# Two adapter layers on one core: outer Strassen-Winograd sums with one operand in PSUM, fixed PSUM banks, and another order of transposes

## The chip, the cores and the metric

The kernel runs on one core of a Trainium2 chip. The metric is the device time of one execution in microseconds; the figure for a kernel is the median of several executions. A separate profiled execution gives the trace, with its own time.

## The reference

128 samples `x[b]` of 128 rows by 1024 columns pass through two layers. In each layer every sample has one of three roles (`itok_B_1_2`, clipped to 0..2), and the role chooses the weights:

```python
h = jnp.einsum('bsh,bhk->bsk', hidden_states, W_down[role]) + b_down[role][:, None, :]
h = jax.nn.gelu(h, approximate=False)
u = jnp.einsum('bsk,bkh->bsh', h, W_up[role]) + b_up[role][:, None, :]
y = hidden_states + u
mean = jnp.mean(y, axis=-1, keepdims=True)
var = jnp.mean(jnp.square(y - mean), axis=-1, keepdims=True)
yn = (y - mean) * jax.lax.rsqrt(var + LN_EPS)
return yn * gamma[role][:, None, :] + beta[role][:, None, :]
```

The second layer is the same with its own weights and reads the first layer's result. Everything is fp32; the inner width is 512.

## The kernel before, in words

The samples are sorted by role on the chip. `perm` holds the order, and 14 groups of eight samples with one role (the octets) are taken together; the few left over go in pairs and singles. A layer has three stages: the left-over items (`PlainItem`), the 14 octets (`Octet`), which make `gelu(x W_down)` transposed and store it to DRAM, and the up stage (`Up`), 65 items that make the second product, the residual sum and the normalization.

**An octet** multiplies the 1024-wide transposed input of eight samples by `W_down`. It does so with two levels of the Winograd form of Strassen's product. The outer level cuts the input into four blocks: A11 and A12 are the first and second half of the 1024 features for samples 0 to 3, A21 and A22 the same for samples 4 to 7. A block is 128 partitions by 2048 numbers (four feature tiles of 512 columns). The input arrives by DMA in a ring of five `staged` buffers (`Turns.load`), and VectorE transposes it in 32x32 squares into the blocks (`Turns.turn`, L557): two instructions of 128x512 for each sample, `k=0` for the first half of the features and `k=1` for the second. Seven blocks exist (`take_block`, `give_block`).

From the four blocks, `Octet.outer` (L651 to L662) makes four outer sums: s3 = A11 - A21, A21 = A21 + A22 in place, s2 = A22 - s3 and s4 = A12 - s2. Each is two instructions of 128x1024; the last half of s4 is GpSimd's, the other seven are VectorE's. Seven outer products B11, B21, T2, T1, T3, B22, T4 (the list `ORDER`) follow, with A11, A12, s2, A21, s3, s4, A22 as left operands (`LEFT`). All but T3 are cut again: GpSimd makes four inner sums d0 to d3 of 128x512 for each (`inner`, L674 to L683), TensorE multiplies seven inner products p1 to p7 (`product`, order `PS`), each two matmuls of 256 columns. T3 is multiplied plainly in eight steps of 512 columns.

**The inner products meet in PSUM.** p1, p3, p5 and p7 add into a "b" bank, p4 and p6 into an "e" bank, and p2 into an "x" bank, into which ScalarE first copies what p1 left (`carry`, L716). `flow` (L734 to L744) takes each finished result out of PSUM, mostly by VectorE, which adds it to `results`, and for B11 by ScalarE copies (L732). As p7 adds to the same bank as p5, it may only start when the flow between them has read the bank. `after` applies the gelu on ScalarE (L722).

**The order of all work is written by hand.** `at(time, step)` puts a step into one list by a nominal time, and the list is run through in order of time, which fixes the order of instructions on each engine; every engine then works in that order and waits only for data. In `Octet.steps`, `put(t, f)` counts in slots of one inner product. An octet is 50 slots: product q begins at slot 0, 7, 14, 21, 28, 36, 43, and its p1 to p7 are two slots apart, so that two outer products are always interleaved. The transposes of the eight samples stand at slots -28 to -4, the outer sums at -1.4 (s3), 3 (s2), 9 (A21) and 15 (s4), the inner sums from 5.6 slots ahead of each product.

**PSUM** has eight banks: a pool gives the tags "b", "e" and "a" three, three and two of them in rotation (`bank`, L143 to L146). The plain items take four banks at a time, the up stage also runs on b, e and a.

**Jobs beside the octets.** The weights of the other two roles are prepared while octets 0 to 11 run: `DownJob` (four sums of 128x1024 at L398, then 24 of 128x256 at L363 to L366) in octets 0 to 3, and three `UpJob` (four sums each at L398) in octets 4 to 11.

Of the kernel before, what the change touches and what calls it, by code (L numbers as in the profile page):

```python
# [10 lines left out]
F32 = mybir.dt.float32  # L11
# [16 lines left out]
def kernel(  # L28
# [113 lines left out]
    nc.gpsimd.memset(zero, 0.0)  # L142
    BANKS = {"b": 3, "a": 2, "e": 3}  # L143

    def bank(t, tag):
        return psum.tile([P, 512], F32, tag=t, name=f"{t}{tag}", bufs=BANKS[t])  # L146

# [3 lines left out]
    def zeros(tags):  # L151
        for t in tags:
            cleared(bank(t, "_zero"))

# [22 lines left out]

    ps = bank("a", "row_ps")
    nc.tensor.matmul(ps[:, 0 : B + 2 * R], ones[0:1, 0:P], row[0:1], start=True, stop=True)
# [66 lines left out]
    def gathered(name, values):  # L246
        ps = bank("a", name + "_ps")
        nc.tensor.matmul(ps[0:SQ, 0:B], values, onehot, start=True, stop=True)
        t = const.tile([1, B], I32, name=name)
        nc.vector.tensor_copy(t, ps[0:1, 0:B])  # L250
        return t, ps
# [122 lines left out]
    class DownJob:  # L374
# [20 lines left out]

        def sum(self, name):
            a, b = {"T1": ("B12", "B11"), "T2": ("B22", "T1"), "T3": ("B22", "B12"), "T4": ("B21", "T2")}[name]
            tt(self.at[name], self.at[a], self.at[b], sub)  # L398

# [3 lines left out]
        def steps(self, start, end):  # L403

            s = [(start - 0.1, self.begin)] + [(start + 0.8 * q, lambda q=q: self.load(q)) for q in range(NQ)]
            work = [(1.0, lambda name=name: self.sum(name)) for name in ("T1", "T2", "T3", "T4")]
            for k, q in enumerate(INNER):
                for op in range(4):
                    work.append((0.35, lambda q=q, k=k, op=op: inner_sums(self.at[q], self.extra[k % 3])[op]()))
                work.append((0, lambda q=q, k=k: self.store(q, k % 3)))  # L410
            work += [(0, lambda q=q: self.store(q, None)) for q in PLAIN]
            t, pace = start + 6, (end - start - 6) / sum(w for w, _ in work)
            for w, step in work:
                s.append((t, step))
                t += w * pace
            return s
# [7 lines left out]
    class UpJob:  # L424
# [18 lines left out]
        def steps(self, start, end):  # L443
            s = [(start - 0.1, self.begin)] + [(start + q, lambda q=q: self.load(q)) for q in range(2)]
            t, pace = start + 6, (end - start - 6) / 4
            for name in ("T1", "T2", "T3", "T4"):
                s.append((t, lambda name=name: DownJob.sum(self, name)))
                t += pace
            for k, name in enumerate(ORDER):
                s.append((end + 0.6 * k, lambda name=name: self.store(name)))  # L450
            return s
# [120 lines left out]
    class PlainItem:  # L572


        def __init__(self, layer, slots, nth, early=False):
            self.layer, self.slots, self.nth, self.early = layer, slots, nth, early
            self.parity = parity = nth % 2
            self.tag = f"p{layer}_{slots[0]}"
            self.turns = Turns(layer, slots)
            self.n = len(slots) * P  # L580
            self.tags = ["e", "b", "a", "e"] if parity else ["b", "e", "a", "b"]

# [9 lines left out]
        def prepare(self):  # L592
            self.bias = new_bias(self.layer, None if self.slots[0] < 2 else self.slots[0], self.tag)
            first = turn_of["results"] % 2
            k = (first, 1 - first, 2)[self.nth % 3]
            self.h = results[:, ts(k, 2048)][:, 0 : 4 * self.n].rearrange("p (f c) -> p f c", f=4)
            self.ps = [bank(t, self.tag + str(f)) for f, t in enumerate(self.tags)]

# [31 lines left out]
    class Octet:  # L630
        def __init__(self, layer, g):
            self.layer, self.g = layer, g
            self.slots = [2 + 8 * g + s for s in range(8)]
            self.tag = f"o{layer}_{g}"
            self.turns = Turns(layer, self.slots)
            self.b = {}
            self.flows = {}

# [6 lines left out]
        def turn(self, s, k):  # L645
            i, c = divmod(s, 4)
            if c == 0:
                self.take(f"A{i + 1}{k + 1}")
            self.turns.turn(s, k, self.b[f"A{i + 1}{k + 1}"][1], c * P)

        def outer(self, name, half, engine):  # L651

            o, a, b, op = {
                "s3": ("s3", "A11", "A21", sub),
                "A21": ("A21", "A21", "A22", add),
                "s2": ("s2", "A22", "s3", sub),
                "s4": ("s4", "A12", "s2", sub),
            }[name]
            if o not in self.b:
                self.take(o)  # L660
            o, a, b = (self.b[n][1][:, ts(half, 2)] for n in (o, a, b))
            engine.tensor_tensor(o, a, b, op)  # L662

        LEFT = {"B11": "A11", "B21": "A12", "T2": "s2", "T1": "A21", "T3": "s3", "B22": "s4", "T4": "A22"}

# [27 lines left out]
        def product(self, q, p):  # L693
            ps, d = self.ps.setdefault(q, {}), self.d[q]
            m = lambda ii, kk: self.m(q, ii, kk)
            if p == "p1":
                ps["b"] = bank("b", self.tag + q)
            elif p == "p4":
                ps["e"] = bank("e", self.tag + q)
            t, w, v = {  # L700
# [10 lines left out]
        def carry(self, q):  # L711
            ps = self.ps[q]
            ps["x"] = bank("a", self.tag + q)
            if self.g == 0 and q in ("B11", "B21"):
                cleared(ps["x"])
# [43 lines left out]
        def plain_step(self, q, k):  # L759
            ps = self.ps.setdefault(q, {})  # L760
            f, j = divmod(k, 4)
            if j == 0:
                ps[f] = bank("e", f"{self.tag}{q}{f}")
            nc.tensor.matmul(
# [34 lines left out]
        def steps(self, base, turns=True):  # L799
# [3 lines left out]
            self.d = {}  # L803
            if turns:
                for s in range(8):
                    t = -28 + 3.3 * s
                    turning.append((base + 0.5 * t, lambda s=s: self.turns.load(s)))
                    for k in range(2):
                        put(t + 0.8 * k, lambda s=s, k=k: self.turn(s, k))
            put(-0.6, self.begin)  # L810
            starts, _ = self.starts()
            put(starts["B21"] - 1, self.begin_0)
            for t, name in ((-1.4, "s3"), (3, "s2"), (9, "A21"), (15, "s4")):
                for half in range(2):
                    engine = nc.gpsimd if name == "s4" and half else nc.vector
                    put(t + 2.2 * half, lambda n=name, h=half, g=engine: self.outer(n, h, g))
            gone = {"A11": ("B11",), "A12": ("B21",), "s2": ("T2",), "A21": ("T1",), "s3": ("T3",), "s4": ("B22",), "A22": ("T4",)}
            for q in ORDER:
                b = starts[q]
                put(b + 13.6, lambda q=q: self.give(self.LEFT[q]))  # L820
                if q in PLAIN:
# [48 lines left out]
    class Up:  # L870
# [40 lines left out]
        def seeded(self, t):  # L911
            ps = bank(t, self.tag)
            if self.m < 3:
                cleared(ps)
# [3 lines left out]
        def products(self):  # L918
# [7 lines left out]
            def s2():  # L926
                ps["a"] = bank("a", self.tag)
                product(ps["a"], A(0, 1), "B21", self.place, True)
                self.end(0, 0, ps["a"])
# [31 lines left out]

            seeds = [(-4, lambda: self.seeded("b")), (1.5 if self.ns == 2 else -0.5, lambda: self.seeded("e"))]
            if self.ns == 2:
# [18 lines left out]
        def finish_last(self):  # L982
# [29 lines left out]
            def begin_bank(item, s, cols, t):  # L1012
                begun[item.m, cols.start] = ps = bank(t, f"{item.tag}_end{cols.start}")
                nc.scalar.copy(ps, item.t["beta"][:, cols])
# [114 lines left out]
    for layer in range(2):  # L1129
# [6 lines left out]
        for kind, n in items:  # L1136
# [6 lines left out]
            else:  # L1143
# [12 lines left out]
                for s in range(len(slots)):  # L1156
                    turning.append((base - lead + 1.7 * s, lambda item=item, s=s: item.turns.load(s)))
                    for k in range(2):
                        at(base - lead + 1.7 * s + 0.4 * k, lambda item=item, s=s, k=k: item.turn(s, k))
                if not first:  # L1160
                    idx = LEFT.index(slots[0])

                    def load(item=item, idx=idx, layer=layer, slot=slots[0], only=None):
                        if not only:
                            item.r = reg(role_at, slot, [ENG.SP], R - 1)
                        c = reg(left_changed, idx, [ENG.SP], 1) if idx >= 2 else None
                        parts = 1 if only is None else 4
                        load_raw(layer, item.parity, item.r, [nc.sync], parts=parts, cond=c, only=only)

# [7 lines left out]
        turning.sort(key=lambda v: v[0])  # L1177
        for k, (time, step) in enumerate(turning):
            when = max(time - 9, turning[k - NSTAGED][0] + 0.45) if k >= NSTAGED else time - 5
            loaded = max(when, loaded)  # L1180
# [30 lines left out]

        o_at = oct_base[0][1]
        job_1 = DownJob(layer, 1, five_blocks, nc.scalar)
        for time, step in job_1.steps(begun_at + 15, o_at - 26):
# [35 lines left out]


        up_base = []
        for m in range(NSEQ):
# [107 lines left out]
```

## Time and profile before

| | us |
|---|---|
| median of three runs (3126.56 to 3132.67) | 3126.98 |
| the profiled execution | 3125.19 |
| its span on the core | 3123.1 |
| layer 0: up to the first product of octet 0 | 155.0 |
| layer 0: the 14 octets | 641.8 |
| layer 0: up stage | 773.2 |
| layer 1: up to the first product of octet 0 | 131.8 |
| layer 1: the 14 octets | 636.4 |
| layer 1: up stage and end | 784.8 |

The time is that of the whole execution, the span what the core's records cover; 2.1 us lie around it. The stage borders were read from the first matmul of the tiles of each octet (for octet g they are named bo_gB, eo_gB, ao_gB and bo_gT, eo_gT, ao_gT in the trace). Engines are PE (TensorE), PEld (its weight loads), DVE (VectorE), ACT (ScalarE), POOL (GpSimd) and SP (which issues the DMAs). A row of a group gives count, busy time and the mean duration of one instruction; an entry in square brackets in a timeline is the idle time ahead of an instruction and what ended it.

| octet, from p1 to the next octet's p1 | layer 0, us | layer 1, us |
|---|---|---|
| 0 | 50.46 | 47.55 |
| 1 | 48.59 | 46.54 |
| 2 | 48.31 | 47.67 |
| 3 | 46.69 | 46.69 |
| 4 to 12, mean | 44.87 | 44.89 |
| shortest of these | 43.88 | 43.88 |

### The profile page before, as it was taken

Reading aid. Unit: us, or ns where it says so; the run is one execution under the profiler, and the core shown is the slowest. Engines: PE = TensorE matmul, PEld = TensorE weight load, DVE = VectorE, ACT = ScalarE, POOL = GpSimd, SP = SyncE. Lnnn points to the kernel's source line nnn. Section 1 sums busy time; section 2 is a strip of 40 time slices with the busy share of each in tenths; the row PEclk is TensorE's granted clock in tenths of the full one; section 3 lists DMA queues with packets and bytes.
Section 4 is the critical chain, followed back from the end, with each engine's and each line's share of the span. In section 5 each row is a group of like instructions: output and inputs, shape, how many; then the busy total and the mean of one; then the engine's idle time right before and its main releaser. Section 6 shows DMA issues by size and latency. Waiting matters only on the chain. (4 is left out here: it accounts for less than half of the span.)

```text
span 3123.1 us, 40323 instructions
## 1 busy us (share of the span) xinstructions
PE 3027.9 (97%) x9953; PEld 1872.6 (60%) x9953; DVE 2434.8 (78%) x3802; ACT 1160.2 (37%) x2576; POOL 2195.6 (70%) x1593
## 2 busy tenths in 40 slices
PE   7889999999999999999998999999999999999999
PEld 6776777778544444444477777778774444444443
DVE  4489989888677777777764899898966777777777
ACT  1122222222445455545421222222224545454544
POOL 0087888898577776777601988888886777767775
PEclk8999999999999999999999999999999999999999
DMA  8765658766667676866688566677658666777665
GB/s 190 219 169 165 195 184 251 210 189 206 246 219 219 221 257 236 281 217 221 220 223 251 140 200 187 198 227 224 186 178 282 216 223 215 269 251 256 216 222 176
DMA packets 350014, 675.42 MB, mean 216 GB/s; under 512 B 35661, under 2 KB 232526, under 8 KB 342618
## 3 DMA queue, kind: packets, MB, share of 16 engines
q1 hardware_dynamic: 338914, 658.63, 68.0%
q10 hardware_dynamic: 10872, 14.22, 1.3%
q8 instruction: 85, 1.39, 0.2%
q14 instruction: 143, 1.17, 0.1%
HBM read 669.55 MB, written 247.49 MB: 294 GB/s over the span
## 5 line engine op out<-in xcount | busy, mean ns | idle before, releaser
L864 PE MATMUL bu<-wall,blocks 128*128 (+1 forms) x2016 | 907.6, 592 | 0.0
L864 PEld LDWEIGHTS bu<-wall,blocks 128*128 128x128 f32 x2016 | 383.0, 190 | 479.6 <-issue 478.2
L1077 POOL TENSOR_TENSOR varu<-varu,mhalf 128x1 f32<-128x1 f32 x254 | 329.9, 1299 | 421.4 <-ACT varu L1076 416.4
L864 PE MATMUL eu<-wall,blocks 128*128 (+1 forms) x1008 | 473.7, 592 | 0.0
L557 DVE STREAM_TRANSPOSE blocks<-staged 128x512 f32<-128x512 f32 x512 | 341.4, 690 | 132.8 <-DMA staged<-in_x_dram 66.5
L1084 DVE SCALAR_TENSOR_TENSOR units<-blocks,meanu,results 128x1024 f32<-128x1024 f32 x249 | 319.8, 1284 | 79.7 <-ACT units L1075 79.5
L662 DVE TENSOR_TENSOR blocks<-blocks 128x1024 f32<-128x1024 f32 x196 | 339.5, 1735 | 0.0
L864 PEld LDWEIGHTS eu<-wall,blocks 128*128 128x128 f32 x1008 | 191.5, 190 | 240.7 <-issue 211.2
L677 POOL TENSOR_TENSOR units<-blocks 128x512 f32<-128x512 f32 x84 | 123.3, 1468 | 291.7 <-DVE blocks L557 257.1
L722 ACT ACTIVATE results<-results,bcolo 128x256 f32<-128x256 f32 x392 | 207.2, 538 | 317.0 <-DVE results L744 286.9
L1071 ACT ACTIVATE partu<-statu 128x2 f32<-128x2 f32 x254 | 51.6, 203 | 716.2 <-DVE blocks L980 711.4
L674 POOL TENSOR_TENSOR units<-blocks 128x512 f32<-128x512 f32 x168 | 265.2, 1578 | 66.0 <-PE bo_3B L689 6.0
L1092 POOL TENSOR_TENSOR units<-units,results 128x1024 f32<-128x1024 f32 x125 | 295.4, 2364 | 2.5 <-ACT units L1091 2.5
L1075 ACT ACTIVATE units<-blocks,meanu 128x1024 f32<-128x1024 f32 x250 | 287.1, 1148 | 8.5
L683 POOL TENSOR_TENSOR units<-blocks,units 128x512 f32<-128x512 f32 x168 | 276.7, 1647 | 6.6
L1094 DVE SCALAR_TENSOR_TENSOR units<-units,varu,results 128x1024 f32<-128x1024 f32 x128 | 279.3, 2182 | 0.0
L972 DVE TENSOR_TENSOR blocks<-bu,blocks 128x512 f32<-128x512 f32 x252 | 173.3, 688 | 133.4 <-PE bu L864 133.4
L864 PE MATMUL au<-wall,blocks 128*128 (+1 forms) x504 | 236.8, 592 | 0.0
L857 POOL TENSOR_TENSOR blocks<-blocks 128x256 f32<-128x256 f32 x126 | 207.5, 1647 | 26.7 <-PE eu L864 26.7
L980 DVE SCALAR_TENSOR_TENSOR blocks<-bu,blocks 128x512 f32<-128x512 f32 x250 | 171.9, 688 | 49.9 <-PE bu L864 49.9
L680 POOL TENSOR_TENSOR units<-units,blocks 128x512 f32<-128x512 f32 x84 | 140.8, 1677 | 62.8 <-PE bo_1T L689 5.0
L864 PEld LDWEIGHTS au<-wall,blocks 128*128 128x128 f32 x504 | 95.8, 190 | 119.4 <-issue 119.0
(779 smaller groups left out, 5274.3 us busy)
## 6 DMA issues: line engine op xcount, KB each, us to landing
staged<-in_x_dram SPq DMA_DIRECT2D x512, 128.0 KB
mid<-units SPq DMA_DIRECT2D x128, 512.0 KB
staged<-mid SPq DMA_DIRECT2D x512, 128.0 KB
blocks<-in_x_dram SPq DMA_DIRECT2D x126, 512.0 KB
blocks<-mid SPq DMA_DIRECT2D x126, 512.0 KB
out_dram<-units SPq DMA_DIRECT2D x125, 512.0 KB
hq<-results SPq DMA_DIRECT2D x56, 1024.0 KB
blocks<-hq SPq DMA_DIRECT2D x112, 512.0 KB
```

What stands on the lines that cost most here:

```text
L557: nc.vector.transpose(to[:, :, at_col : at_col + P].rearrange("p j (a t) -> p j a t", t=SQ), v[:, ts(k, 4)])
L662: engine.tensor_tensor(o, a, b, op)
L674: engine.tensor_tensor(d["d1"], m(0, 0), m(1, 0), sub)
L683: engine.tensor_tensor(d["d2"], m(0, 1), d["d0"], sub)
L722: nc.scalar.activation(y, y, AF.Gelu, bias=self.bias[:, f : f + 1])
L857: engine.tensor_tensor(dst[:, 1], a11, a21, sub)
L864: nc.tensor.matmul(ps, a[:, j], wu(w, place, j), start=start and j == 0, stop=j == 1, skip_group_check=True)
L1075: nc.scalar.activation(box["o"], self.x[:, s], AF.Square, bias=m, accum_out=v)
L1077: nc.gpsimd.tensor_tensor(v, v, mhalf[:, 0:1], ALU.pow)
L1084: nc.vector.scalar_tensor_tensor(box["o"], self.x[:, s], box["m"][:, 0:1], self.t["gamma"], add, mul)
L1092: nc.gpsimd.tensor_tensor(o, o, self.t["beta"], add)
L1094: nc.vector.scalar_tensor_tensor(o, o, v, self.t["beta"], mul, add)
```

## The change

Outer sums. They go sample by sample (128 partitions by four runs of 128 columns), 16 instructions of 512 elements in place of eight of 1024. For samples 4 to 7 the transpose of the first half (A21 as it comes) is written to a PSUM bank instead of a block, and s3 and A21 read it there. For s2, ScalarE copies the sample's piece of A22 into a PSUM bank, and for s4 (made in place in A12) it copies s2 of samples 4 and 5; the last two pieces of s4 are GpSimd's with all operands in SBUF.

Order. From octet 1 on, samples 0 to 3 are transposed at slots -42.5 to -30 and samples 4 to 7 at -22 to -5; s3 stands at slots -15 to -4, A21 at -8.2 to -1.2, s2 at 0 to 5.1, s4 at 22 to 27. Octet 0 has slots of its own. The jobs' sums are cut in halves of 512.

Banks. Eight tiles are held for good, and each role has a fixed set: in the octets b has three, e two (was three), x one (was two), and two are for the raw transposes and ScalarE's copies.

```diff
-    BANKS = {"b": 3, "a": 2, "e": 3}
...
+    all_banks = [psum.tile([P, 512], F32, tag=f"bank{k}", name=f"bank{k}", bufs=1) for k in range(8)]
+    BANKS = {"b": (0, 1, 2), "e": (3, 4, 5), "a": (6, 7), "de": (3, 4), "dt": (5, 7)}
+    bank_turn = dict.fromkeys(BANKS, 0)
+
+    def bank(t):
+        k = BANKS[t][bank_turn[t] % len(BANKS[t])]
+        bank_turn[t] += 1
+        return all_banks[k]
...
-        def sum(self, name):
+        def sum(self, name, half):
             a, b = {"T1": ("B12", "B11"), "T2": ("B22", "T1"), "T3": ("B22", "B12"), "T4": ("B21", "T2")}[name]
-            tt(self.at[name], self.at[a], self.at[b], sub)
+            n = self.at[name].shape[1] // 2
+            o, a, b = (self.at[k][:, ts(half, n)] for k in (name, a, b))
+            tt(o, a, b, sub)
...
-            self.ps = [bank(t, self.tag + str(f)) for f, t in enumerate(self.tags)]
+            self.ps = [all_banks[k] for k in ((2, 3, 4, 6), (5, 7, 0, 1))[self.parity]]
...
         def turn(self, s, k):
             i, c = divmod(s, 4)
+            if i and k == 0:
+                self.raw21[s] = v = bank("dt").rearrange("p (j c) -> p j c", c=P)
+                self.turns.turn(s, k, v, 0)
+                return
...
+        def copied(self, name, s):
+
+            self.copy[s] = v = bank("dt").rearrange("p (j c) -> p j c", c=P)
+            nc.scalar.copy(v, self.at_sample(name, s))
+
+        def outer(self, name, s, apart=True):
+
+            v = lambda n: self.at_sample(n, s)
+            if name == "s3":
+                tt(v("s3"), v("A11"), self.raw21[s], sub)
+            elif name == "A21":
+                tt(v("A21"), self.raw21[s], v("A22"), add)
+            elif name == "s2":
+                tt(v("s2"), self.copy[s], v("s3"), sub)
+            elif apart:
+                tt(v("A12"), v("A12"), self.copy[s], sub)
+            else:
+                nc.gpsimd.tensor_tensor(v("A12"), v("A12"), v("s2"), sub)
+
+        LEFT = {"B11": "A11", "B21": "A12", "T2": "s2", "T1": "A21", "T3": "s3", "B22": "A12", "T4": "A22"}
...
-                ps["e"] = bank("e", self.tag + q)
+                ps["e"] = bank("de")
...
-            ps["x"] = bank("a", self.tag + q)
-            if self.g == 0 and q in ("B11", "B21"):
+            ps["x"] = all_banks[6]
+            if self.g == 0 and q == "B11":
                 cleared(ps["x"])
...
-                    t = -28 + 3.3 * s
-                    turning.append((base + 0.5 * t, lambda s=s: self.turns.load(s)))
-                    for k in range(2):
-                        put(t + 0.8 * k, lambda s=s, k=k: self.turn(s, k))
+                    if early:
+                        first, second, s3, a21 = (
+                            (-42.5 + 1.8 * s, -36 + 2 * s, None, None)
+                            if s < 4
+                            else (
+                                (-22, -21, -15, -8.2), (-19.5, -18.5, -13.5, -7.4), (-11, -7, -6, -2.5), (-9.5, -5, -4, -1.2)
+                            )[s - 4]
+                        )
+                    else:
+                        t = -29 + 3.3 * s if s < 4 else -13.2 + 2.6 * (s - 4)
+                        first, second, s3, a21 = t, t + 0.8, t + 1.7, max(t + 2.4, -8.2 + 0.8 * (s - 4))
+                    turning.append((base + 0.5 * first, base + 0.5 * second, lambda s=s: self.turns.load(s)))
+                    for t, k in zip((first, second), (0, 1) if s < 4 else (1, 0)):
+                        put(t, lambda s=s, k=k: self.turn(s, k))
+                    if s >= 4:
+                        put(s3, lambda s=s: self.outer("s3", s))
+                        put(a21, lambda s=s: self.outer("A21", s))
...
-            for t, name in ((-1.4, "s3"), (3, "s2"), (9, "A21"), (15, "s4")):
-                for half in range(2):
-                    engine = nc.gpsimd if name == "s4" and half else nc.vector
-                    put(t + 2.2 * half, lambda n=name, h=half, g=engine: self.outer(n, h, g))
...
+            for s in range(4, 8):
+                t = ((-1.4, 0, 2, 3.7) if self.g else (1.2, 2.4, 3.6, 4.8))[s - 4]
+                put(t, lambda s=s: self.copied("A22", s))
+                put(t + 1.4, lambda s=s: self.outer("s2", s))
+                t = 21 + 1.6 * (s - 4)
+                if s < 6:
+                    put(t, lambda s=s: self.copied("s2", s))
+                put(t + 1.3, lambda s=s: self.outer("A12", s, s < 6))
             for q in ORDER:
                 b = starts[q]
-                put(b + 13.6, lambda q=q: self.give(self.LEFT[q]))
+                if q != "B21":
+                    put(b + 13.6, lambda q=q: self.give(self.LEFT[q]))
...
-            if self.m < 3:
+            if self.m < 4:
                 cleared(ps)
...
-            seeds = [(-4, lambda: self.seeded("b")), (1.5 if self.ns == 2 else -0.5, lambda: self.seeded("e"))]
+            seeds = [({0: -3.4, 37: -2.9}.get(self.m, -4), lambda: self.seeded("b")), (1.5 if self.ns == 2 else -0.5, lambda: self.seeded("e"))]
...
-        for k, (time, step) in enumerate(turning):
-            when = max(time - 9, turning[k - NSTAGED][0] + 0.45) if k >= NSTAGED else time - 5
+        for k, (time, _, step) in enumerate(turning):
+            when = max(time - 9, turning[k - NSTAGED][1] + 0.05) if k >= NSTAGED else time - 5
...
+        at(o_at - 0.1, lambda: bank_turn.update(b=0, de=1))
```

## The prediction

> **What bounds the kernel now.** I read the busy shares first, then the stages, the octets one by one, TensorE's waits inside an octet, and last what VectorE and GpSimd do at those moments. The page's first row, and busy time by stage (columns: length of the stretch; then busy us and instructions of each engine; the TensorE clock; DMA):
>
> ```profile
> PE 3027.9 (97%) x9953; PEld 1872.6 (60%) x9953; DVE 2434.8 (78%) x3802; ACT 1160.2 (37%) x2576; POOL 2195.6 (70%) x1593
> 155.00:796.80 641.80, 615.25 (x2569) 486.69 (x2568) 562.40 (x852) 168.36 (x405) 544.76 (x354) 0.99 0.64 193
> 796.80:1570.00 773.20, 773.20 (x1820) 345.11 (x1819) 588.84 (x894) 387.95 (x827) 541.82 (x432) 1.00 0.72 237
> 1701.80:2338.20 636.40, 613.86 (x2569) 486.48 (x2568) 561.15 (x852) 168.80 (x405) 545.78 (x354) 0.99 0.68 193
> ```
>
> TensorE is the bound. In the up stage (second row) it never pauses, so no VectorE work saved can show there. In the two octet stages it is idle for 26.6 and 22.5 us by the records, while VectorE is 88% and GpSimd 85% busy. The change is in these stages. Single octets:
>
> ```profile
> 254.05:302.36 48.31, 44.33 (x185) 34.46 (x184) 47.67 (x72) 12.01 (x29) 37.96 (x25) 1.00 0.59 188
> 529.55:575.14 45.59, 44.20 (x186) 34.55 (x184) 42.00 (x62) 12.00 (x29) 38.76 (x25) 1.00 0.73 226
> 708.99:752.88 43.89, 43.39 (x185) 34.88 (x184) 37.90 (x60) 12.09 (x29) 38.24 (x25) 1.00 0.50 145
> ```
>
> Octet 2, with the DownJob's sums, is VectorE's: 47.67 of 48.31 us. Octets 8 and 12 are not, but still lose something to waits. TensorE's timeline shows the floor and the losses:
>
> ```profile
> 575.14 1.03 PE L689 MATMUL bo_9B<-blocks,wall 128*128 128x256 f32 x4
> 594.13 1.03 PE L689 MATMUL bo_9T<-units,wall 128*128 128x256 f32 x4
> 541.18 1.13 PE L689 MATMUL bo_8B<-blocks,wall 128*128 128x256 f32 x4 [0.42 <-DVE results L734]
> 544.70 1.10 PE L689 MATMUL bo_8B<-units,wall 128*128 128x256 f32 x4 [0.67 <-DVE results L744]
> 597.37 1.13 PE L689 MATMUL bo_9T<-units,wall 128*128 128x256 f32 x4 [0.49 <-POOL units L680]
> ```
>
> The first two rows are 22 slots apart without a wait between: 18.99 / 22 = 0.863 us a slot, so 50 slots are 43.2 us. 28 octets would take 1209; they take 641.8 + 636.4 = 1278.2. All that this change can win is about 69 us. The other rows name the two culprits: a flow of VectorE that came late, near an octet's start, and GpSimd's d0 for T1 at slot 25. What the two engines do then:
>
> ```profile
> 538.62 2.17 DVE L662 TENSOR_TENSOR blocks<-blocks 128x1024 f32<-128x1024 f32 x1
> 540.72 0.41 DVE L734 TENSOR_TENSOR results<-bo_8B,results 128x256 f32<-128x256 f32 x1
> 541.89 2.33 DVE L662 TENSOR_TENSOR blocks<-blocks 128x1024 f32<-128x1024 f32 x1
> 544.15 0.41 DVE L744 TENSOR_TENSOR results<-bo_8B,results 128x256 f32<-128x256 f32 x1
> 543.10 2.25 POOL L683 TENSOR_TENSOR units<-blocks,units 128x512 f32<-128x512 f32 x1
> 548.87 2.35 POOL L662 TENSOR_TENSOR blocks<-blocks 128x1024 f32<-128x1024 f32 x1
> ```
>
> Each late flow sits right behind an outer sum of more than 2 us; TensorE's two waits end when it is read. And the sums are this long only in company:
>
> ```profile
> L662 DVE TENSOR_TENSOR blocks<-blocks x196: 1182/1948/2343, 163.1 to 2306.9; 128x1024 f32<-128x1024 f32 x196
> L683 POOL TENSOR_TENSOR units<-blocks,units x168: 1262/1526/2312, 152.8 to 2330.4; 128x512 f32<-128x512 f32 x168
> L557 DVE STREAM_TRANSPOSE blocks<-staged x512: 661/698/714, 18.4 to 2291.1; 128x512 f32<-128x512 f32 x171
> L972 DVE TENSOR_TENSOR blocks<-bu,blocks 128x512 f32<-128x512 f32 x252 | 173.3, 688 | 133.4 <-PE bu L864 133.4
> L915 ACT COPY bu<-results x130: 572/574/590, 791.1 to 3086.7; 128x512 f32<-128x512 f32 x130
> ```
>
> (The three figures are shortest, median and longest in ns.) An outer sum takes 1.18 us alone and 1.95 typically, a GpSimd sum 1.26 or 2.3, and transposes and sums out of PSUM hardly vary. VectorE sums with two SBUF operands and GpSimd sums wait for one another.
>
> **The change, part by part, for an octet.**
>
> Outer sums. Removed: VectorE's seven, 12.06 us an octet (measured over layer 0), and GpSimd's one, 2.5. Added: 14 of 512 on VectorE, one operand in PSUM. The nearest row is L972 (688 ns, the same size, the same kind of operands, with GpSimd 70% busy): 14 x 0.688 = 9.63, saving 2.4. Bounds: two halves of the lone 1.18 with no fixed part, 8.3, and the old 12.06 without any gain. GpSimd gets 2 x 1.27 = 2.5, no change. [...]
>
> GpSimd's inner sums. 24 x 1.27 + 2.35 = 32.8 us without company, 38.9 measured: 6 us of waiting. The outer sums are 340 us of VectorE's sums with two SBUF operands in these stages; L740, L775 and the jobs are some 240. So I take 59% of the 6 off, 3.5; bounds 0 and 6. GpSimd's s4 half moves from slot 17, amid T1's inner sums (the 2.35 at 548.87), to slots 25 to 27, during T3, which has none. That removes the wait for d0.
>
> ScalarE's copies. Six of 0.575 = 3.5 us on an engine with 12 of 45 busy. The cover is ScalarE's idle time; what could be late is s2 behind the copy, which is the rival below.
>
> Transposes into PSUM. Eight an octet change their destination. No row has VectorE write PSUM; ScalarE's does it in 574 ns for the same 512. I take 0.69, as to SBUF; bounds 0.57 and twice, 1.38.
>
> Order. Over slots -2 to 7 VectorE now has four outer sums (1.2 to 2.0 each, 7 us) among the flows of two products, and no idle time. After it has four s2 sums there, 2.75 us. The s3 and A21 sums (5.5) take the place of the 8 transposes (5.5) that move into slots 7 to 20, where A21 and s4 (some 5.7) stood. So no stretch gets fuller. The moved transposes bring their loads along on SP's queue; a load still follows the release of its ring buffer, and nothing more is queued between. A12's transposes at slot 14 of the octet before need A11's block, through with TensorE at 13: margin 0.9 us, behind it the flows of B21. Today's similar wait (L557 for GpSimd's s4, 1.6 us at its longest) goes.
>
> Banks, at nothing. x has one: p2 ends at slot 7, its flow (0.41) and the next carry (0.36) must be done before p3 at slot 11: 3.45 - 0.77 = 2.7 us spare. e has two: the tightest is B22's p4 after T3's first half, three slots less a flow of 0.69: 1.9 spare. VectorE's single instructions stay under that. If they don't, each such miss stalls TensorE by the excess.
>
> Job sums in halves: 40 x about 0.15 more on VectorE = 6 us in all, most under idle time. Up stage: one more clearing pair in each layer, under 1 us; left at 0.
>
> **The sum.** Octets 4 to 13: now 895.7 for 20. VectorE at about 37.5 (39.95 - 2.4), GpSimd at 35.4 (38.9 - 3.5) of 43.2, both known waits gone; the best octet of today (43.88) has 0.7 of waiting; I leave half: 43.5 x 20 = 870, -25.7. Octets 1 to 3: now 284.5 for 6. Octet 2's VectorE work becomes 47.67 - 13.24 + 9.63 = 44.1, which still bounds; with 0.6 of gaps 44.7, x 6 = 268, -16.3. Octet 0: now 98.0 for 2. In layer 0 VectorE waits for staged input (3.5, 0.9, 1.1 us) and then TensorE 5.8 us for VectorE, which does five outer sums ahead of the flow (5.72). With seven halves left (4.8) and flows between them, I take 2.5 off each: -5. Total -47. Profiled execution 3125.2 - 47 = 3078; the median runs 1.8 higher: **3080 us**. From the bounds (all 69 won; half the early octets' gain missing and 0.5 a steady octet left) 3060 to 3094.
>
> **Rivals.** (a) Half the gain: the early octets stay where they are, because the jobs' sums with two SBUF operands still meet GpSimd, and the tight blocks cost 0.3 an octet. -47 + 16 + 8 = -23: 3104. For it: in octet 2 the 256-wide job sums at L363 take 1.17 us. Against: GpSimd has less to meet them with.
>
> (b) Slower, by ScalarE as a new link in VectorE's queue. s2 waits for a copy; ScalarE works in order and is itself waiting, up to 3.6 us at a time, for VectorE's flows (L722). If at an octet's start the copies come 1.3 us late four times, VectorE stands still 5.2 us with the flows of T4 and B11 behind it, and TensorE with it: 43.2 + 0.3 + 5.2 = 48.7 in all but the two first, less a cover of 1.5: 47.2 x 26 + 98 = 1325, +47: 3174. It decides from about 0.8 us late each time. Against: ScalarE is some 30% busy there. Equal in effect are transposes into PSUM at 1.38: +5.5 VectorE an octet, octets 1 to 3 at 49.6, octets 4 to 13 at 45.5 (as octet 8 now, with 42.0 of VectorE), +27: 3154; from about 1.2 us each.
>
> (c) No change: the waits named are not what paces the octets, but GpSimd's chain of inner sums behind T3 and T1, unshortened: 3127.
>
> [...]
>
> **Chances.** Forecast 0.57, (a) 0.24, (b) 0.15, (c) 0.04. A difference under 0.2% (6 us, the spread of the three runs) can't be told from none. Faster 0.81, same 0.04, slower 0.15. The range, 3060 to 3120, holds the forecast and (a) and leaves out 0.19.
>
> **What would show it.** Right: VectorE's outer sums near 690 ns each, PSUM transposes near 690, GpSimd sums near 1.3, octets 4 to 13 at 43.2 to 43.7, no wait of TensorE for L734 or L744 at an octet's start. Wrong: VectorE waiting for ScalarE's copies ahead of s2, TensorE for the x or e bank, transposes above 1 us; or octets at 43.3 with a time above 3100, when another stage would have lost it.

## The result, and the profile after

The changed kernel takes 3112.47 us (median of six runs, 3111.03 to 3116.51) against 3128.36 for the kernel before beside it: a ratio of 0.9949, 95% interval 0.9937 to 0.9961. That is 16 us won. The forecast was 47: the direction was right, the size was off by a factor of three. The profiled execution took 3111.03 us with a span of 3109.2. Its busy shares:

```profile
PE 3021.5 (97%) x9955; PEld 1869.1 (60%) x9955; DVE 2374.4 (76%) x4038; ACT 1239.9 (40%) x2744; POOL 2056.1 (66%) x1621
```

VectorE works 60 us less and GpSimd 140 us less than before, the span is only 14 us shorter. So the work went and the waits did not all go with it. Single instructions (shortest, median and longest in ns; L677 is s3, L681 s2, L567 the transposes into PSUM, L706 GpSimd's d2):

```profile
L677 DVE TENSOR_TENSOR blocks<-blocks,bank x112: 661/672/689, 154.3 to 2278.5; 128x512 f32<-128x512 f32 x112
L681 DVE TENSOR_TENSOR blocks<-bank,blocks x112: 669/679/693, 165.9 to 2285.0; 128x512 f32<-128x512 f32 x112
L567 DVE STREAM_TRANSPOSE bank<-staged x112: 676/711/721, 153.6 to 2277.6; 128x512 f32<-128x512 f32 x112
L706 POOL TENSOR_TENSOR units<-blocks,units x168: 1262/1276/1733, 154.3 to 2314.6; 128x512 f32<-128x512 f32 x168
```

These three prices of the forecast hold: 0.69 for an outer sum and 0.69 for a transpose were taken, GpSimd near 1.3. The loss must be in where the work lies. In the changed kernel all PSUM tiles are called "bank", so octets are measured from the first matmul of T3 (slot 28) to that of the next octet. Summed over both layers:

| stretch | before, us | after, us | difference |
|---|---|---|---|
| first product to T3 of octet 0 | 57.95 | 63.70 | +5.7 |
| T3 of octet 0 to T3 of octet 1 | 95.69 | 96.68 | +1.0 |
| T3 of octet 1 to T3 of octet 3 | 190.96 | 182.60 | -8.4 |
| T3 of octet 3 to T3 of octet 13 | 895.57 | 881.52 | -14.1 |
| T3 of octet 13 to the last product | 51.15 | 51.14 | 0 |

The octet stages give 15.7; in the rest of the span 1.8 is lost again. The octets fall into two kinds. From one T3 to the next, five of the 12 intervals from octet 1 on take 43.39 to 43.44 us in layer 0, the floor of TensorE; two of them have no job sums, two have them behind slot 50 only, and one has a single one in slots 28 to 50. All intervals with two or more job sums in slots 28 to 50, and one with a single one, take 43.9 to 45.8. Three of TensorE's waits (over the whole run the lines that end them cost 15.5, 8.1 and 4.9 us; T3's own matmuls wait 6.8 more for L757, a flow of VectorE):

```profile
168.38 1.19 PE L712 MATMUL bank<-units,wall 128*128 128x256 f32 x2 [8.11 <-ACT results L755]
293.42 1.10 PE L712 MATMUL bank<-blocks,wall 128*128 128x256 f32 x4 [1.19 <-DVE results L795]
301.94 1.10 PE L712 MATMUL bank<-units,wall 128*128 128x256 f32 x4 [0.53 <-ACT bank L739]
```

The first is in octet 0: TensorE stops at slot 5 for ScalarE's flow of B11 (L755). The second is B22's p4, which needs an e bank that T3's first half holds until VectorE's L795 has read it. The third is a p3 behind the carry into the one x bank. What VectorE does ahead of the second one:

```profile
289.16 1.18 DVE L763 TENSOR_TENSOR results<-results 128x256 f32<-128x256 f32 x1
290.26 1.48 DVE L368 TENSOR_TENSOR wall<-wall 128x256 f32<-128x256 f32 x1
291.67 0.41 DVE L761 TENSOR_TENSOR results<-bank,results 128x256 f32<-128x256 f32 x1
292.00 0.67 DVE L677 TENSOR_TENSOR blocks<-blocks,bank 128x512 f32<-128x512 f32 x1
292.60 0.68 DVE L795 TENSOR_TENSOR results<-bank,results 128x512 f32<-128x512 f32 x1
```

No gap between them, and a job's sum (L368, 1.48 us for 256 columns) in the row. Busy time by half octet (length; PE, PEld, DVE, ACT, POOL; clock; DMA). First the kernel before, slots 28 to 50 and 50 to 78 from T3 of octet 11, where no job runs:

```profile
690.04:709.00 18.96, 18.96 (x74) 13.69 (x73) 17.61 (x30) 4.29 (x10) 15.66 (x12) 1.00 0.74 250
709.00:733.93 24.93, 24.43 (x113) 21.19 (x112) 20.29 (x30) 7.80 (x19) 22.59 (x14) 1.00 0.75 211
```

Then the changed kernel, the same halves of the same octet, and those from T3 of octet 2, where the DownJob runs:

```profile
683.29:702.40 19.11, 19.11 (x73) 13.42 (x72) 18.23 (x32) 3.73 (x8) 14.02 (x11) 1.00 0.83 281
702.40:726.68 24.28, 24.28 (x114) 21.37 (x113) 17.07 (x37) 11.13 (x27) 19.11 (x16) 1.00 0.52 174
283.46:302.60 19.14, 17.42 (x64) 11.76 (x63) 18.78 (x31) 2.98 (x7) 13.19 (x11) 1.00 0.48 146
302.60:329.30 26.70, 26.61 (x123) 22.86 (x122) 24.29 (x49) 12.06 (x29) 20.71 (x17) 1.00 0.67 224
```

Before, the third number (DVE) was 93% of the first half and 81% of the second. After, it is 95% and 70%: the change emptied the half that had room and filled the one that had little. With a job it is 98% and 91%: a job sum in the first half has nowhere to go.

### The profile page after: what moved, and what is told of

The parts are those of the page before. It is cut to its first block, busy times and chain, and to the rows that moved or that the text cites. A ratio compares the mean times of both kernels' runs of the same rounds, so it can differ in the third digit from the quotient of the medians.

```text
span 3109.2 us, 40816 instructions
## 1 busy us (share of the span) xinstructions
PE 3021.5 (97%) x9955; PEld 1869.1 (60%) x9955; DVE 2374.4 (76%) x4038; ACT 1239.9 (40%) x2744; POOL 2056.1 (66%) x1621
## 5 line engine op out<-in xcount | busy, mean ns | idle before, releaser
L905 PE MATMUL bank<-wall,blocks 128*128 (+1 forms) x3528 | 1519.3, 592 | 0.0
L905 PEld LDWEIGHTS bank<-wall,blocks 128*128 128x128 f32 x3528 | 670.1, 190 | 839.7 <-issue 803.8
L712 PE MATMUL bank<-units,wall 128*128 128x256 f32 x2352 | 562.2, 382 | 20.3 <-ACT results L755 15.5
L712 PE MATMUL bank<-blocks,wall 128*128 128x256 f32 x2352 | 563.3, 381 | 12.3 <-DVE results L795 8.1
L712 PEld LDWEIGHTS bank<-blocks,wall 128*128 128x128 f32 x2352 | 443.3, 190 | 134.6 <-issue 47.1
L712 PEld LDWEIGHTS bank<-units,wall 128*128 128x128 f32 x2352 | 447.1, 191 | 127.0 <-issue 56.6
L1013 DVE TENSOR_TENSOR blocks<-bank,blocks 128x512 f32<-128x512 f32 x378 | 260.4, 689 | 214.0 <-PE bank L905 212.9
L1021 DVE SCALAR_TENSOR_TENSOR blocks<-bank,blocks 128x512 f32<-128x512 f32 x500 | 339.9, 686 | 68.4 <-PE bank L905 68.1
L767 DVE TENSOR_TENSOR results<-bank,results 128x256 f32<-128x256 f32 x672 | 270.9, 408 | 124.8 <-PE bank L712 118.8
L567 DVE STREAM_TRANSPOSE blocks<-staged 128x512 f32<-128x512 f32 x400 | 274.9, 696 | 106.7 <-DMA staged<-in_x_dram 57.8
L610 PE MATMUL bank<-blocks,wall 128*128 128x256 f32 (+1 forms) x1152 | 233.4, 366 | 36.0 <-DMA wall<-in_L_cond_W_down_dram 28.0
L610 PEld LDWEIGHTS bank<-blocks,wall 128*128 128x128 f32 x1152 | 205.1, 196 | 65.9 <-issue 29.7
```

The costliest lines, as they stand in the source:

```text
L567: nc.vector.transpose(to[:, :, at_col : at_col + P].rearrange("p j (a t) -> p j a t", t=SQ), v[:, ts(k, 4)])
L610: nc.tensor.matmul(self.ps[f][:, 0 : self.n], raws[self.parity][:, j, ts(f, P)], self.v[:, j, 0 : self.n], start=j == 0, stop=j == 7, skip ...
L712: nc.tensor.matmul(ps[:, 0:256], u, v[:, j], start=start and j == 0, stop=stop and j == 1, skip_group_check=True)
L767: tt(o, ps, beta if q == "B21" and first else o, add)
L905: nc.tensor.matmul(ps, a[:, j], wu(w, place, j), start=start and j == 0, stop=j == 1, skip_group_check=True)
L1013: nc.vector.tensor_tensor(y, ps, y, add)
```

## The experiments

The theory has two parts. **Place**: the job sums meet a VectorE that is full in slots 28 to 50, and the smaller sets of banks turn its lateness into waits. **Copies**: octet 0 is lost to ScalarE's copies. The rivals are the banks alone, the late input of octet 0, and VectorE's total.

**Octet 0 without ScalarE's copies of A22** (`if self.g:` ahead of `copied("A22", s)`):

```diff
-                tt(v("s2"), self.copy[s], v("s3"), sub)
+                tt(v("s2"), self.copy[s] if self.g else v("A22"), v("s3"), sub)
```

> The changed kernel, but in octet 0 of each layer VectorE reads A22 for s2 from SBUF and ScalarE copies nothing for it. Theory (ScalarE's copies wait for the late A21 sums, B11's flows stand behind them on ScalarE, and TensorE stops at slot 5 for 8.1 and 7.4 us): both waits for L755 go, octet 0 gets some 6 us shorter in each layer, time near 3101 (3097 to 3105). Rival (octet 0 waits for its late input anyway, the copies only happen to be in front): the stall moves to T2's inner sums or to B21's flows at its full size, time 3110 to 3113.

Measured: 3110.14 us, ratio 0.9935 (0.9919 to 0.9952). The waits for L755 went, and waits of 6.06 and 4.72 us for L757, VectorE's first flow of B21, came in their place, four to five slots later. From the first product to T3 of octet 0 it is 30.06 and 29.31 us, against 32.79 and 30.91 with the copies and 30.52 and 27.43 before. But the interval from T3 of octet 0 to T3 of octet 1 gave 2 back in layer 0. The time is the rival's: ScalarE's copies stop TensorE early, and behind them VectorE does. In layer 0 its last long wait for input ends at 158.07 us, and from there it works almost without a gap (0.19 us) until that flow at 169.65. How much of this is the late input and how much VectorE's own order is not separated here. In the changed kernel the copies looked like this:

```profile
163.45 0.59 ACT L671 COPY bank<-blocks 128x512 f32<-128x512 f32 x1 [6.23 <-DVE blocks L679]
166.00 0.59 ACT L671 COPY bank<-blocks 128x512 f32<-128x512 f32 x1 [1.96 <-DVE blocks L679]
166.53 0.37 ACT L755 COPY results<-bank 128x256 f32<-128x256 f32 x1
```

The copy waits for a bank that VectorE's A21 sum (L679) still reads, and the flow that TensorE needs stands behind it on ScalarE.

**T3's first half in a b bank:**

```diff
-                ps[f] = bank("de")
+                ps[f] = bank("de" if f else "b")
```

> The changed kernel, but the first half of T3's plain product goes to a b bank instead of an e bank, so that in T3's stretch three banks share what two did. Theory (with two e banks TensorE waits for T3's flows, 8.1 us for L795 and 6.8 for L757 by the profile): these waits go, the octets with 1.2 us of wait come to 43.4 to 43.9, time near 3100 (3098 to 3104). Rival (VectorE is late for its own reasons, and the wait moves on to the next bank or sum): under 4 us, time 3108 to 3113.

Measured: 3125.04 us, 0.9983 (0.9974 to 0.9993): by the ratios some 11 us worse than the change, which neither theory had. The wait of 1.19 went, as meant. TensorE then ran on to T4's p3, where the x bank's carry was as late as ever, and stood 2.15 us in one piece. Two stretches around that wait, in octet 2 (the clock is third from the end):

```profile
302.10:305.20 3.10, 1.02 (x5) 0.57 (x3) 3.10 (x5) 0.42 (x2) 3.10 (x3) 1.00 0.00 0
305.28:308.70 3.42, 3.42 (x10) 2.61 (x11) 3.42 (x9) 1.66 (x4) 0.22 (x1) 0.67 0.93 290
```

Over the 3.4 us after the pause TensorE's granted clock is 0.67 in the mean, and 10 matmul records fit where some 16 do at full clock. Shorter windows show two values: 1.00 for the first 1.2 us, then 0.50 from 306.47 to 309.88. From octet 0's T3 to the end of the octets, both layers together, this run has five such stretches of 3.41 us at 0.50, the changed kernel one. At some 1.7 us lost in each, the four more are about 7 of the 11 us, an estimate from these figures. The two intervals between the T3s of octets 1 and 3 took 47.7 to 48.0 us each instead of 45.5 to 45.8. Here a wait taken away ahead of a later one with the same cause was no gain, and one long wait cost more than two short ones (1.19 and 0.53 us in the changed kernel, above).

**Both edits:**

> Both edits of the two runs before it: octet 0 without ScalarE's copies of A22, and T3's first half in a b bank. If the two losses are separate, their gains add: near 3089 (3085 to 3095). If one hides behind the other, the time is that of the better single one, 3099 to 3104.

Measured: 3116.45 us, 0.9955 (0.9939 to 0.9972). Neither. Octet 0 profits from both (T3 to T3 47.38 in layer 0, against 51.63 and 50.28 with one of them), octets 1 to 3 lose as in the run before.

**The banks alone**, on the kernel before: the changed kernel's whole set of banks (in the octets `"de": (3, 4)` for e and bank 6 for x; the plain items and the up stage also have theirs), with outer sums, order and job sums as they were.

> The kernel before, with its outer sums, order of transposes and whole job sums, but with the changed kernel's banks: two e banks and one x bank in the octets, the other two left idle. Theory (fewer banks turn VectorE's lateness into waits of TensorE): slower than the kernel before by 5 to 20 us, with waits for the flows of T3. Rival (banks cost nothing by themselves, as I had predicted): within 3 us of the kernel before.

Measured: 3131.80 us, 1.0009 (1.0000 to 1.0019). 2.7 us slower, hardly told from nothing: the rival. Fewer banks cost little where VectorE's time lies as it did.

**Whole job sums** (the halves undone):

> The changed kernel with the jobs' four sums whole (1024 columns) as before, instead of in halves. Theory (VectorE has no idle time in slots 28 to 50 of an octet, and a flow that comes late there becomes a wait for a bank): a whole sum of up to 1.9 us in front of a flow makes the waits of octets 1, 2, 4, 5, 8 and 9 longer, some of them long enough to lower TensorE's clock: slower than the changed kernel by 5 to 15 us, 3117 to 3128. Rival (the halves matter little, as I had predicted): within 3 us of 3112.

Measured: 3106.34 us, 0.9937 (0.9920 to 0.9954; the profiled execution was 3113.43). Not slower, and outside both expectations: the theory was wrong on this point, and it is not the length of the single sum that costs the time. In the profiled execution, which is 7 us above the other three, octets 4 and 5 came to 44.1 and 44.2 (45.0 and 45.4 in halves), while intervals with whole sums only behind slot 50 rose to 43.9 and 44.0 (43.4), and the interval behind octet 0's T3 got 2.6 to 2.7 longer.

**No job sums** (left out are the sums that prepare the weights of two roles):

> The changed kernel without the sums of the jobs beside the octets (DownJob of place 2 and the UpJobs; their loads and stores stay, one small clearing of their room is added at the start), so that the weights of two roles are wrong. Theory (what octets 1 to 13 still lose is VectorE's job sums meeting the two e banks and the one x bank): every octet from 1 on at 43.4 us, and the wait of 3.7 us in octet 0 of layer 0 gone: near 3085 (3082 to 3090). Rival (the waits belong to the new order itself): the octets with waits keep more than half of them, above 3100.

Measured: 3080.28 us, 0.9854 (0.9837 to 0.9870). All intervals from T3 of octet 0 on are 43.39, but one of 44.04. So, but for 0.6 us, everything that octets 1 to 13 still lost hangs on the job sums; the order, the banks and the copies lose nothing there by themselves. From the first product to T3 of octet 0 it is 63.7 us over both layers, as in the changed kernel: that part of the loss does not hang on them.

**The job sums in slots 5 to 27**, the half with room. The jobs' nominal times are spread over these slots of the octets that the job had, and the DownJob begins them in octet 1:

```diff
+            (max(start, o_at + n * OCT + 2.5), min(end, o_at + n * OCT + 13.5)) for n in range(NOCT)
```

> The changed kernel with the jobs' sums moved to slots 5 to 27 of the octets, where VectorE was 78% busy, out of slots 28 to 50, where it was 96% busy. Theory (it is the place of the sums, not their amount): most of the waits go, octets at 43.4 to 44, time near 3092 (3088 to 3100). Rival (VectorE's total is the limit in these octets, 42.0 of 45.5 us): the waits move to the octets' first half, above 3105.

Measured: 3083.13 us, 0.9865 (0.9849 to 0.9882), with the same sums as the changed kernel, and below the theory's range. Octet 1 in this kernel, its two halves and the whole:

```profile
230.90:249.90 19.00, 19.00 (x72) 13.32 (x71) 18.18 (x33) 3.73 (x8) 15.91 (x13) 1.00 0.30 93
249.90:274.72 24.82, 24.62 (x114) 21.38 (x113) 23.73 (x47) 11.04 (x27) 18.44 (x14) 1.00 0.61 208
230.90:274.72 43.82, 43.62 (x185) 34.71 (x184) 41.90 (x79) 14.77 (x35) 34.35 (x27) 1.00 0.48 158
```

VectorE is 96% busy in both halves, and the octet takes 43.82 us. The octet from 283.46 above had 43.07 us of VectorE work in 45.84. So the total was not the limit: the place was. Nor did the sums get cheaper by moving: all job sums together keep VectorE busy for 153.6 us here and 156.0 in the changed kernel.

**No copies by ScalarE**: s2 and VectorE's pieces of s4 read SBUF alone.

```diff
-                tt(v("s2"), self.copy[s], v("s3"), sub)
+                tt(v("s2"), v("A22"), v("s3"), sub)
-                tt(v("A12"), v("A12"), self.copy[s], sub)
+                tt(v("A12"), v("A12"), v("s2"), sub)
```

> The changed kernel, but s2 and VectorE's two pieces of s4 read both operands from SBUF and ScalarE copies nothing into PSUM; s3 and A21 still read the raw transposes in PSUM. Theory (a VectorE sum with two SBUF operands waits for GpSimd and holds it up): these six sums go from 0.68 to some 1.0 to 1.3 us, GpSimd's from 1.28 to above 1.4, octets without jobs from 43.4 to 43.6 to 44.5: 3115 to 3130. Rival (the PSUM operand is worth nothing here, TensorE being the bound): 3108 to 3113, the lower end for octet 0 without the wait for copies.

Measured: 3120.77 us, 0.9983 (0.9973 to 0.9992), some 11 us worse than the change. s2 in this kernel:

```profile
L681 DVE TENSOR_TENSOR blocks<-blocks x112: 662/1420/1782, 167.5 to 2295.3; 128x512 f32<-128x512 f32 x112
```

As fast as from PSUM when alone, twice as long in the middle, more than the theory's 1.0 to 1.3. The 34 of these that overlap no GpSimd instruction take 662 to 686 ns; the 42 that one covers for over nine tenths of their time take 1417 to 1782. In the changed kernel 74 of the 112 are covered so, and take 669 to 693. GpSimd's d2 (L706) grew from a mean of 1310 ns to 1377, with the same median of 1276, short of the theory's 1.4 us. But octets without jobs stayed at 43.42: what TensorE loses is again in the octets with jobs.

**The same move on the kernel before** (its whole job sums in slots 5 to 27):

> The kernel before the change, with its whole job sums moved to slots 5 to 27 of the octets in the same way. Theory (the jobs' place costs the old kernel too, but its octets without jobs need 43.9 to 45 by themselves, since long outer sums stand in front of the flows at an octet's start): octets 1 to 3 near 45, the rest 44 to 45, time 3108 to 3120. Rival (the place of the jobs is the whole story and PSUM is worth nothing): near 3085.

Measured: 3146.63 us, 1.0060 (1.0043 to 1.0076): slower, outside both expectations. The two intervals between the T3s of octets 1 and 3 took 50.3 to 52.0 us each instead of 46.7 to 49.9. In the kernel before this row, slots 50 to 64, shows one reason:

```profile
709.00:720.80 11.80, 11.80 (x56) 10.40 (x55) 11.71 (x15) 4.40 (x11) 9.69 (x5) 1.00 0.81 244
```

VectorE is busy for 11.71 of 11.80 us at an octet's start, with its long outer sums. The rest of that half had room, but there GpSimd is busy too (22.59 of 24.93 us over the half, above), and VectorE's total rose by 26 us in this run (2461.0 against 2434.8) with as many instructions. Which of the two weighs more was not tested. The changed kernel has more room in this half (17.07 of 24.28 us busy, for 20.29 of 24.93), and did not use it.

**Versions with the jobs moved.** First octet 0 without the copies of A22, then also with its s2 sums behind VectorE's first flow of B21 (slot 10.2) and T2's inner sums at slots 10.6 to 14.2, then no copies at all:

```diff
-                put(t + 1.4, lambda s=s: self.outer("s2", s))
+                put(t + 1.4 if self.g else 10.2 + 0.1 * (s - 4), lambda s=s: self.outer("s2", s))
```

> The changed kernel with the jobs' sums in slots 5 to 27 and octet 0 without ScalarE's copies of A22. Theory (without job sums in octet 0 the earlier loss behind it is gone, and the 2 to 3 us of its first part remain won): 3 to 5 us below the version with the jobs moved alone, near 3079. Rival (the late input sets octet 0 whatever the order): the same as with the jobs moved alone, 3081 to 3085.

> As the run before it, and in octet 0 the four s2 sums stand behind the first VectorE flow of B21 (slot 10.2 instead of 2.6 to 6.2), GpSimd's inner sums of T2 at slots 10.6 to 14.2. Theory (TensorE's wait in octet 0 is for that flow, which stands behind the sums on VectorE): the 6 us wait splits or shrinks, near 3075. Rival (T2's inner sums need s2 as soon, the wait moves to T2 at its size): within 2 us of the run before it.

> The changed kernel with the jobs' sums in slots 5 to 27, and s2 and VectorE's pieces of s4 from SBUF alone, no copies by ScalarE. Theory (with the jobs out of the way VectorE and GpSimd have room for the longer sums; octets without jobs took 43.4 us in the run without copies): octets at 43.4 to 43.9, time 3078 to 3086. Rival (sums with two SBUF operands make flows late again): octets above 44, time above 3092.

Measured: 3078.68 us, 0.9839 (0.9823 to 0.9856); 3077.32, 0.9842 (0.9826 to 0.9859); 3089.09, 0.9873 (0.9857 to 0.9890). The first comes near what was expected of it, though its interval and that of the version with the jobs moved alone overlap. In the second, TensorE's waits for that flow fall from 10.6 to 6.0 us in the two layers, while GpSimd's T2 sums cost 2.2; by the time the two are not to be told apart, as the rival had it. The third lies between its two expectations: without copies the three intervals up to T3 of octet 3 take 45.3 to 46.0 us (43.4 to 44.4 with them), the others 43.42 to 43.8. By their ratios the first two versions are 1.1% below the changed kernel, some 33 us.

## Why the prediction was wrong

**What bounds the kernel.** Right, but for the floor of an octet. The up stage did not move. 18.99 / 22 slots gave 43.2 us; the octets without any wait take 43.39, so that 5 of the 69 us that could be won were not there.

**The outer sums, GpSimd's inner sums, the transposes into PSUM.** Right in mechanism, and in size but for GpSimd, which gained more than was taken: 0.67 to 0.68 us for 0.688, 0.711 for 0.69, GpSimd's busy time down 140 us for 3.5 x 28 = 98. The wait for d0 went. Two halves from PSUM take 1.36 us (2 x 0.68), more than the 1.18 of one whole sum alone; VectorE did not lose by it, since the whole sums took 1.95 us in company.

**Order: "So no stretch gets fuller", and the job sums "most under idle time".** This is the step that failed. I compared the sums that moved with the transposes that moved, and never measured how busy VectorE was in each half of an octet. Without jobs, slots 28 to 50 went from 93% to 95%, slots 50 to 78 from 81% to 70%: the first half got 0.6 us more work and the second 3.2 us less. The job sums stayed in the half that had won nothing, where there was no idle time left for them. Left out they give 3080.28, moved 3083.13, so that by the ratios their place costs 26 us and all of them 30. The price was off as well: 80 halves keep VectorE busy for 79.1 us and 40 whole sums for 56.9, which is 22 us more where an estimate of 6 was taken.

That the version with the jobs moved comes near the 3080 forecast is in part luck. Up to T3 of octet 1 it wins nothing over the kernel before (154.1 us for 153.6, over both layers), where the sum has at least 5 us; from T3 of octet 1 to T3 of octet 3 it wins 16.5, more than the sum has there; from there to T3 of octet 13 it wins 26.9, for 25.7.

**Banks, at nothing.** Right for what it said, as the run with the banks alone shows (+2.7 us, interval reaching 0). Its condition did not hold with the jobs there: "VectorE's single instructions stay under that" counted one instruction of lateness, but several followed one another without a gap, and 1.9 us of slack at B22's p4 were used up. A sign of being wrong that I had named, TensorE waiting for the x or e bank, is what the profile after shows.

**Octets 1 to 3: -16.3.** From T3 of octet 1 to T3 of octet 3, four of these six, it is -8.4, where -10.9 is their share. Each has four job sums in slots 28 to 50 and takes 45.5 or 45.8, for the 44.7 of the sum; with the jobs moved they take 43.8 and 43.4.

**Octets 4 to 13: -25.7.** Came out near -14 (T3 of octet 3 to T3 of octet 13). Some 10 of the 14 are the lower floor, 43.39 for the best 43.88 before, 20 times; little of what the job sums cost was won. I set all 20 at 43.5. Ten of the intervals there are at 43.4 and two at 43.9; the other eight, all with UpJob sums in slots 28 to 50, are at 44.5 to 45.4.

**Octet 0: -5.** The sign was wrong. From the first product to T3 of octet 1 it is +6.7 over both layers. The +5.7 up to T3 of octet 0 are in the main the copies: 59.4 us without them, 63.7 with them, 57.95 before. The rest up to T3 of octet 1 is again the job sums, 96.7 us as they stand and 88.7 with them moved. I counted VectorE's sums and did not follow ScalarE's queue there, though rival (b) named the mechanism: a copy that waits, flows behind it. I placed that rival in the octets with early transposes, where it did not happen (VectorE waited for copies 3.7 us in all of octets 1 to 13 of layer 0); it happened where the input is late.

**Rivals.** (a), at 3104, was nearest to the time of the three, and half right in its reason: octets 1 to 3 kept some 2 us each above the floor because of job sums, but moving them took most of this away with the sums as long as before, so that it was their place. That octet 0 got longer, (a) did not have; its number is near by luck. (c) fell. The change in halves brought nothing by itself: the run with whole sums is no slower.

Not tried: other slots for the jobs on the kernel before, and a third e bank or second x bank beside the raw transposes, for which none of the kernel's eight bank tiles is left.

## What to carry to other kernels

Where an order is written by hand, make the table of each engine's busy share by slot, for the order before and the order after, and put every background job into the slot with room; a total that fits does not help a stretch that is full. Room in the mean of a half may not be enough either: in the kernel before, the first 11.8 us of the half with room were full, and the same move made it slower. An instruction added to an engine's ordered list is priced by what can make it wait and by what stands behind it, separately for the first pass of a loop, where inputs can come late: octet 0 took 59.4 us up to T3 without ScalarE's copies of A22 and 63.7 with them, over both layers. Before removing a wait, look for the next one with the same cause: here its removal made one long pause (2.15 us) of two short ones (1.19 and 0.53 us), and that was dearer, by some 11 us in all.

## What the runs showed of the hardware

In the run with T3's first half in a b bank, a pause of TensorE of 2.15 us was followed by a granted clock of 0.67 in the mean over 3.4 us: 1.00 at first, then 0.50 for 3.41 us (above). In the kernel before, a wait of 1.82 us in layer 1 (to 1809.00) was followed by 0.50 from 1809.09 to 1812.50, and one of 1.48 us with another of 0.20 behind it (to 216.60 and 217.91) by 0.50 from 218.48 to 221.89. But three waits of 1.71 us (to 260.24, 308.55 and 1849.74) were each followed by 3.41 us of full clock. Behind the pair of waits, and behind the second of these three:

```profile
217.90:221.40 3.50, 3.49 (x10) 2.81 (x11) 2.35 (x5) 0.37 (x1) 3.50 (x3) 0.58 0.99 291
308.55:312.00 3.45, 3.45 (x16) 3.06 (x17) 3.45 (x4) 1.51 (x4) 0.74 (x1) 1.00 0.95 230
```

So the length of a single pause does not tell in these runs whether the clock falls behind it.

A VectorE sum of 128x512 with an operand in PSUM (s2 in the changed kernel) took 669 to 693 ns, also where a GpSimd instruction covered it; with both operands in SBUF it took 662 to 686 ns where none overlapped it and 1417 to 1782 where one covered it. In the kernel before, the outer sums of 128x1024 on VectorE took 1182 to 1221 ns where no GpSimd sum overlapped them (18 of 196) and 1955 in the median where one covered over nine tenths of them (128). GpSimd's sums at L683 took 1264 to 1282 ns where no VectorE sum with both operands in SBUF overlapped them (55 of 168) and 2252 in the median where an outer sum covered over half of them (29). In these runs the worth of the PSUM operand was in not meeting GpSimd.
